# A graph network on one core: the last step of the last pair of batches by halves of the nodes, and the whole order of work drawn anew

## Chip, cores and metric

The kernel runs on one NeuronCore of one Trainium2 chip. The metric is the device time of one execution in microseconds (us), the median of several runs. Everything is in float32.

## What is computed

`x` has 32 batches of 512 nodes by 128 channels and `adj` is one 512 x 512 matrix, the same for all batches and used for both adjacencies of each layer. The reference, cut to what matters:

```python
# layer 0: x_1 stands for x; W[k] = weight of the k-th of 7 parts
parts = [x_1, adj x_1, adj^2 x_1, adj^3 x_1, adj x_1, adj^2 x_1, adj^3 x_1]
x = layernorm(x + sum_k parts[k] @ W[k])

# layer 1: five steps of a gated update, h starts as x
def step(h):
    m  = adj @ h                       # m_in and m_out are the same, since both matrices are adj
    av = concatenate([m, m])
    u3 = h @ u3_w.T + u3_b
    z  = sigmoid(av @ w3_w.T + w3_b + u3)
    r  = sigmoid(av @ w4_w.T + w4_b + u3)
    hv = tanh(av @ w5_w.T + w5_b + (r * h @ u5_w.T + u5_b))
    return (1 - z) * h + z * hv
x = layernorm(x + step^5(x))
```

## The kernel before

The 32 batches are 16 *pairs* (`q` = 0 to 15); each pair goes through layer 0 and then five steps (`s` = 0 to 4). The engines are TensorE (PE), VectorE (DVE), ScalarE (ACT), GpSimd (POOL) and SyncE (SP), the last of which only issues transfers. A float32 matmul is two PE instructions in the profile, so each count of PE instructions is twice that of the matmuls (transposes, L290, are one each).

**Products.** The products with `adj` (`pair_product`, `seven`, L380 to L550; L511 is the matmul line) take two batches together as a 2 x 2 block scheme with seven products in place of eight; the sums that it needs are made by POOL (L498) into `S`, and the results are put together by ACT (L372) and DVE (L376) from PSUM into the tiles `m`, one per batch. Layer 0 has similar products (L615, L749, L811).

**One step of one batch** (`gates`, L881): with channels on the partitions and the 512 nodes along the free dimension, `u3s` times `hT` is made in a PSUM bank of its own (L970) and copied with its bias to a tile `uT` by ACT (L975). Then PE makes `w4s m` (r), `w3s m` (z) and `w5s m` (h) in the banks `pr`, `pz`, `ph` (L888, 128 x 512 each). DVE adds bias and `uT` to the r and z banks (L893, L900), ACT takes the sigmoids (L895, L902), DVE makes `rh = r * h` (L896), PE adds `u5s rh` to the h bank (L888), ACT takes tanh (L909), DVE and POOL form the new `hT` (L921, L923, L925). The next product needs `h` with nodes on the partitions; `turn` (L332) does that through DRAM: a block transpose on DVE (L347), four stores issued by SP (L339), one fetch (L345). In the last two steps of the last two pairs (`ON_PE = {14: 2, 15: 2}`) it is done on PE instead (L1019, counted under L290, and a copy on ACT, L1022).

**The last step of pairs 14 and 15** is `quick`: ACT also makes 1 - z from the z bank (L914), DVE makes `(1 - z) h` and `z hv` (L916, L918), and `finish` (L928) lets PE sum three things in one bank by matmuls with the identity (L936): the batch's layer-0 result `h0`, `(1 - z) h` transposed, and `z hv` transposed, four blocks of 128 x 128 each.

**The norm** (`norm`, L292): for each block of 128 nodes two DVE instructions for mean and variance (L301, L302); then POOL, for all four blocks together, adds epsilon (L305), takes the power -1/2 (L308, 128 x 4), and makes the shift (L307, L310); then ACT applies it block by block (L318). For the very last tile DVE applies it (L314) and POOL leaves out the shift. SP stores the whole batch, 256 KB, with one transfer (L953).

**The order** is not written out by hand. `Plan` (L45) takes every operation with its engine, a duration, what it comes after, which buffers it takes and gives back, and a key. `run` goes through planned time: each engine that is free emits its ready operation of lowest key whose buffers are free. What it emits is each engine's order, fixed in the program. The keys are `KEYS[q]` for a pair plus 19 (`LONG`) per step, and small offsets inside a step. Besides real buffers there are tokens: `two` limits how many seven-product schemes are open at once, `inside` how many pairs.

Of the kernel before, what the change touches and what calls it, by code (L numbers as in the profile page):

```python
# [9 lines left out]
F32 = mybir.dt.float32  # L10
AF = mybir.ActivationFunctionType
ALU = mybir.AluOpType
PSUM = bass.MemoryType.PSUM

P = 128
NK = 4
N = NK * P
H = NK // 2
HN = N // 2
# [1 line left out]
NR = P // R  # L21
STEPS = 5
ON_PE = {14: 2, 15: 2}
KEYS = [8.0, 22.0, 60.0, 88.0, 108.0, 144.0, 174.0, 188.0, 210.0, 244.0, 274.0, 310.0, 338.0, 368.0, 384.0, 396.0]
LONG = 19.0
KEPT = 3
FIRST = 2
# [97 lines left out]
def gnn_resnorm_kernel(  # L125
# [17 lines left out]
    nc = tc.nc  # L143
    NP = x.shape[0] // 2
# [7 lines left out]
    def tiles(tag, n, shape=(P, N), pool=work):  # L152
        return [pool.tile(list(shape), F32, tag=f"{tag}_{i}", name=f"{tag}_{i}") for i in range(n)]
# [12 lines left out]
        hT=tiles("hT", 8),  # L166
        X=tiles("X", 3),
        uT=tiles("uT", 6),
        rh=tiles("rh", 2),
        z=tiles("z", 3),  # L170
        m=tiles("m", 5),
        S=tiles("S", 2, (P, 7, H, P)),
        v=tiles("v", 4),
        two=[None] * 3,
        inside=[None] * 14,
    )
    plan = Plan(slots)

    def chunk(k):
        return slice(k * P, (k + 1) * P)  # L180
# [49 lines left out]
    for i, n, of in (  # L230
# [8 lines left out]
        def emit(b11=b11, b12=b12, b21=b21, b22=b22, t=t):  # L239
            for j, (a, b) in enumerate(((b12, b11), (b22, t(0)), (b22, b12), (b21, t(1)))):  # L240
                nc.vector.tensor_tensor(t(j), a, b, ALU.subtract)  # L241
# [40 lines left out]
    ub3s, ub5s = plain(ub3, "ub3s"), plain(ub5, "ub5s")  # L282
    hv_b = const.tile([P, 1], F32, tag="hv_b", name="hv_b")
    hv_ready = plan("DVE", 0.1, lambda: nc.vector.tensor_tensor(hv_b, b5s, ub5s, ALU.add), after=ready, key=-30.0)
    weights = ready + [hv_ready]

    def transposes(dst, src_of):
# [1 line left out]
        for k in range(NK):  # L289
            nc.tensor.transpose(dst[:, chunk(k)], src_of(k), ident)  # L290

    def norm(n, name, src_of, dst_of, after, give, key, by_dve=False):  # L292

        mv = small.tile([P, n, 2], F32, tag="mv", name=f"mv_{name}")
        rstd = small.tile([P, n], F32, tag="rstd", name=f"rstd_{name}")
        shift = small.tile([P, n], F32, tag="shift", name=f"shift_{name}")
        got = []

        def moments(i):
            st = small.tile([P, 6], F32, tag="st", name=f"st_{name}_{i}")  # L300
            nc.vector.bn_stats(st, src_of(i))  # L301
            nc.vector.bn_aggr(mv[:, i, :], st)  # L302

        def power():
            nc.gpsimd.tensor_scalar(rstd, mv[:, :, 1], EPS, None, ALU.add)  # L305
            if not by_dve:
                nc.gpsimd.tensor_scalar(shift, mv[:, :, 0], -1.0, None, ALU.mult)  # L307
            nc.gpsimd.tensor_tensor(rstd, rstd, mhalf[:, :n], ALU.pow)  # L308
            if not by_dve:
                nc.gpsimd.tensor_tensor(shift, shift, rstd, ALU.mult)  # L310

        def apply(i):
            if by_dve:
                nc.vector.tensor_scalar(  # L314
                    dst_of(i), src_of(i), mv[:, i, 0:1], rstd[:, i : i + 1], ALU.subtract, ALU.mult
                )
                return
            nc.scalar.activation(  # L318
                dst_of(i), src_of(i), AF.Identity, bias=shift[:, i : i + 1], scale=rstd[:, i : i + 1]
            )  # L320

        for i in range(n):
            got.append(plan("DVE", 0.48, lambda i=i: moments(i), after=after, key=key))
        p = plan("POOL", 1.2 if by_dve else 1.75, power, after=got, key=key)
        engine, us = ("DVE", 0.35) if by_dve else ("ACT", 0.5)
        over = []
        for i in range(n):
            ends = give if i == n - 1 else []
            over.append(plan(engine, us, lambda i=i: apply(i), after=[p] + over, give=ends, key=key))
        return over  # L330

    def turn(src_of, dst_of, name, after, key, take=(), give=()):  # L332
# [548 lines left out]
    def gates(name, m, h, after, u_done, quick, key):  # L881
# [43 lines left out]
        emit = lambda: nc.gpsimd.tensor_tensor(plan[h], plan[z], plan[h], ALU.add)  # L925
        return plan("POOL", 1.27, emit, after=[t], give=[("z", z)], key=key + 0.8)

    def finish(q, b, name, h, parts, h0_of, after, key, done):  # L928

        bn, z = f"bt{name}", f"z{name}"  # L930
        y = lambda k: plan[bn][:, chunk(k)]

        def summed(tile, turned, first, last):
            for k in range(NK):
                a = tile(k)
                nc.tensor.matmul(  # L936
                    y(k),
                    lhsT=a if turned else ident,
                    rhs=ident if turned else a,
                    start=(first and k == 0),  # L940
                    stop=last,
                    skip_group_check=True,
                )

        keep, new = parts
        emit = lambda: summed(lambda k: h0_of(b)[:, k, :], False, True, False)
        t = plan("PE", 0.44, emit, after=list(after), take=[("bank", bn)], key=key)
        emit = lambda: summed(lambda k: plan[h][:, chunk(k)], True, False, False)
        t = plan("PE", 0.44, emit, after=[t, keep], give=[("hT", h)], key=key)
        emit = lambda: summed(lambda k: plan[z][:, chunk(k)], True, False, True)  # L950
        t = plan("PE", 0.44, emit, after=[t, new], give=[("z", z)], key=key)
        over = norm(NK, f"1_{2 * q + b}", y, lambda k: h0_of(b)[:, k, :], [t], [("bank", bn)], key + 10, q == NP - 1 and b == 1)
        emit = lambda: nc.sync.dma_start(out[2 * q + b].rearrange("(p k) c -> p k c", k=NK), h0_of(b))  # L953
        done.append(plan("SP", 0.36, emit, after=over, key=key + 10, late=2.0))

    def pair(q, key0):
# [6 lines left out]
        for s in range(STEPS):  # L963
            key = key0 + 30.0 + LONG * s
            name = f"{q}_{s}"
            last = s == STEPS - 1
            u_done = []
            for b in range(2):
                bn, uT = f"bv{name}_{b}", f"uT{name}_{b}"
                emit = lambda bn=bn, hb=h[b]: nc.tensor.matmul(  # L970
                    plan[bn], lhsT=u3s, rhs=plan[hb], start=True, stop=True
                )
                take = [("bank", bn), ("uT", uT)]
                p = plan("PE", 0.86, emit, after=h_done[b] + weights, take=take, key=key + 5)
                emit = lambda bn=bn, uT=uT: nc.scalar.activation(plan[uT], plan[bn], AF.Identity, bias=ub3s)  # L975
                u_done.append(plan("ACT", 0.69, emit, after=[p], give=[("bank", bn)], key=key + 5))
# [26 lines left out]
            for b in range(2):  # L1003
                nm = f"{name}_{b}"
                Xb = f"X{nm}"
                quick = last and not by_dma
                d = gates(nm, f"m{nm}", h[b], got[b], u_done[b], quick, key + 10)
                if quick:
                    finish(q, b, nm, h[b], d, h0_of, read[b], key + 15, done)
                    h_done.append(list(d))  # L1010
                    continue
                h_done.append([d])
                give = [("hT", h[b])] if last else []
                if by_dma:
                    h_of = lambda hb=h[b]: plan[hb].rearrange("p (k r l) -> p r k l", r=NR, k=NK)
                    t = turn(h_of, lambda Xb=Xb: plan[Xb], nm, [d] + read[b], key + 15, [("X", Xb)], give)
                else:
                    bn = f"bt{nm}"
                    emit = lambda bn=bn, hb=h[b]: transposes(plan[bn], lambda k: plan[hb][:, chunk(k)])  # L1019
                    take = [("bank", bn), ("X", Xb)]  # L1020
                    t = plan("PE", 0.44, emit, after=[d] + read[b], take=take, give=give, key=key + 15)
                    emit = lambda bn=bn, Xb=Xb: nc.scalar.copy(plan[Xb], plan[bn])  # L1022
                    t = plan("ACT", 0.59, emit, after=[t], give=[("bank", bn)], key=key + 15)
                after.append([t])
                if not last:
                    continue

                y = lambda b=b: h0_of(b)
                emit = lambda b=b, X_new=X_new, y=y: nc.gpsimd.tensor_tensor(
                    fit(y(), True), X_new(b), fit(y(), True), ALU.add  # L1030
                )
                ready = [t, fetched] if q < NP - KEPT else [t]
                t = plan("POOL", 1.27, emit, after=ready, give=[("X", Xb)], key=key + 17)
                i = 2 * q + b
                y_of = lambda k, y=y: y()[:, k, :]
                over = norm(NK, f"1_{i}", y_of, y_of, [t], [], key + 17)
                emit = lambda i=i, y=y: nc.sync.dma_start(out[i].rearrange("(p k) c -> p k c", k=NK), y())
                stored = plan("SP", 0.36, emit, after=over, key=key + 17, late=2.0)
                done.append(stored)
# [62 lines left out]
```

## Time and profile before

| | |
|---|---|
| median of 5 runs | 1511.73 us (1510.98 to 1512.60) |
| profiled execution | 1511.94 us |
| its span (first to last instruction) | 1510.1 us |
| TensorE clock granted, mean | 0.999 |
| PE / DVE / ACT / POOL busy | 99% / 68% / 50% / 56% of the span |
| matmuls of the gates and `u3s` (L888, L970) in the chain that ended last | 36.4% + 9.1% |
| products with `adj` (L511) in that chain | 32.9% |
| bytes moved by DMA | 142.91 MB, mean 95 GB/s |

In the profile's rows, "out<-in" names the tile written and the tiles read, without buffer numbers; "x16" is a count of instructions. The columns of a group are its total busy time and the mean of one instruction in nanoseconds, then the idle time of the engine just before them and what ended it. A row of waits gives the total, how often, and the longest. A row of the chain gives its start, its length and what ran. Ends of matmuls are modelled, so the time from one start to the next is the better measure of what one costs.

### The profile page before, as it was taken

The page shows a single profiled execution, that of the slowest core. Times are in us where ns is not written, and L with a number is a line of the kernel's source. Part 1 is how long each engine was busy: PE and PEld are TensorE (multiplying, and loading weights), DVE is VectorE, ACT ScalarE, POOL GpSimd, SP SyncE. Part 2 cuts the span into 40 slices and gives each one's busy share as a digit, 9 for nine tenths or more (in the row PEclk, how much of TensorE's full clock was granted, in tenths as well). Part 3 has the DMA queues.
Part 4 walks back from the last instruction along what each step waited for, and adds up shares of the span by engine and source line. Part 5 has one row for each costly group of instructions (what it writes and reads, how often), then busy time and mean ns, then how long its engine had stood idle before and what let it go on. Part 6 is the DMA issues. An engine that isn't in the chain of part 4 may idle for free.

```text
span 1510.1 us, 21208 instructions
## 1 busy us (share of the span) xinstructions
PE 1493.9 (99%) x6590; PEld 1045.4 (69%) x6590; DVE 1021.2 (68%) x2123; ACT 749.5 (50%) x1582; POOL 844.4 (56%) x1201
## 2 busy tenths in 40 slices
PE   8999999999999999999999999999999999999997
PEld 7877667667676767676767667677776776665665
DVE  5566676775776667665775766776578665767665
ACT  3354554455445545554454554554545544555454
POOL 4846754665545856663664655655665643544442
PEclk9999999999999999999999999999999999999999
DMA  3213334243333425233333443443343223433310
GB/s 96 71 57 98 100 88 113 79 123 99 98 112 91 119 81 144 80 110 91 98 98 98 119 114 89 111 133 92 98 106 102 80 70 80 108 102 82 84 36 35
DMA packets 165888, 142.91 MB, mean 95 GB/s; under 512 B 18960, under 2 KB 127504, under 8 KB 165776
## 3 DMA queue, kind: packets, MB, share of 16 engines
q1 hardware_dynamic: 165776, 141.57, 33.8%
q8 instruction: 52, 0.85, 0.2%
q14 instruction: 60, 0.49, 0.1%
HBM read 71.76 MB, written 69.73 MB: 94 GB/s over the span
## 4 chain that ended last, share of the span: by engine, by line
PE 98%; DVE 1%; DMA 0%; ACT 0%; POOL 0%; issue 0%; SPq 0%; POOLq 0%; DVEq 0%
PE bank L888 36%; PE bank L511 33%; PE bank L970 9%; PE bank L811 7%; PE bank L749 6%; PE bank L615 5%; PE bank L936 1%; PE bank L447 1%; PE bank L290 1%; DMA xg<-in_x 0%; DVE TT L241 0%; ACT h L318 0%; DVE h L440 0%; POOLq L1098 0%; DVE h L314 0%
## 5 line engine op out<-in xcount | busy, mean ns | idle before, releaser
L925 POOL TENSOR_TENSOR hT<-z,hT 128x512 f32<-128x512 f32 x156 | 198.3, 1276 | 256.9 <-DVE z L923 247.1
L511 PE MATMUL bank<-T,S 128*128 128x256 f32 x1232 | 307.0, 379 | 0.0
L511 PEld LDWEIGHTS bank<-T,S 128*128 128x128 f32 x1232 | 228.4, 190 | 74.9 <-ACT m L372 32.1
L372 ACT COPY m<-bank 128x256 f32<-128x256 f32 x320 | 119.3, 373 | 286.9 <-PE bank L511 285.0
L511 PE MATMUL bank<-at,S 128*128 128x256 f32 x824 | 211.2, 379 | 0.0
L511 PEld LDWEIGHTS bank<-at,S 128*128 128x128 f32 x824 | 153.5, 190 | 57.3 <-issue 37.1
L376 DVE TENSOR_TENSOR m<-bank,m 128x256 f32<-128x256 f32 x240 | 100.7, 420 | 120.3 <-PE bank L511 86.3
L921 DVE TENSOR_TENSOR bank<-bank,hT 128x512 f32<-128x512 f32 x156 | 108.3, 695 | 108.2 <-ACT bank L909 107.4
L888 PE MATMUL bank<-m,w4s 128*128 128x512 f32 x320 | 159.7, 592 | 0.0
L888 PE MATMUL bank<-m,w3s 128*128 128x512 f32 x320 | 157.4, 592 | 0.0
L888 PE MATMUL bank<-rh,u5s 128*128 128x512 f32 x320 | 156.9, 592 | 0.0
L970 PE MATMUL bank<-hT,u3s 128*128 128x512 f32 x320 | 156.5, 592 | 0.0
L893 DVE SCALAR_TENSOR_TENSOR bank<-bank,b4s,uT 128x512 f32<-128x512 f32 x160 | 119.9, 752 | 52.8 <-PE bank L888 48.5
L888 PE MATMUL bank<-m,w5s 128*128 128x512 f32 x320 | 155.0, 592 | 0.0
L909 ACT ACTIVATE bank<-bank,hv_b 128x512 f32<-128x512 f32 x160 | 105.5, 662 | 90.3 <-PE bank L888 89.0
L895 ACT ACTIVATE bank<-bank 128x512 f32<-128x512 f32 x160 | 93.2, 584 | 102.6 <-DVE bank L893 102.5
L975 ACT ACTIVATE uT<-bank,ub3s 128x512 f32<-128x512 f32 x160 | 109.8, 688 | 59.2 <-PE bank L970 58.0
L902 ACT ACTIVATE z<-bank 128x512 f32<-128x512 f32 x160 | 94.3, 596 | 64.8 <-DVE bank L900 60.6
L900 DVE SCALAR_TENSOR_TENSOR bank<-bank,b3s,uT 128x512 f32<-128x512 f32 x160 | 118.6, 752 | 11.3 <-PE bank L888 10.0
L347 DVE STREAM_TRANSPOSE v<-hT 128x512 f32<-128x512 f32 x152 | 105.7, 701 | 13.1 <-POOL hT L925 10.7
L896 DVE TENSOR_TENSOR rh<-bank,hT 128x512 f32<-128x512 f32 x160 | 107.5, 680 | 8.3 <-ACT bank L895 7.8
L376 DVE TENSOR_TENSOR UY<-bank,UY 128x256 f32<-128x256 f32 (+1 forms) x117 | 54.5, 467 | 81.1 <-PE bank L749 35.2
(163 smaller groups left out, 2503.7 us busy)
## 6 DMA issues: line engine op xcount, KB each, us to landing
d<-v SPq DMA_DIRECT2D x832, 64.0 KB, 1.8
X<-d SPq DMA_DIRECT2D x152, 256.0 KB, 2.7
v<-d SPq DMA_DIRECT2D x56, 256.0 KB, 2.8
xg<-in_x SPq DMA_DIRECT2D x32, 256.0 KB, 2.9
out<-h SPq DMA_DIRECT2D x32, 256.0 KB, 2.0
hd<-h SPq DMA_DIRECT2D x13, 512.0 KB, 3.8
h<-hd SPq DMA_DIRECT2D x13, 512.0 KB, 3.8
at<-in_adjT SPq DMA_DIRECT2D x4, 256.0 KB, 5.1
```

The costliest lines, as they stand in the source:

```text
L372: return "ACT", COPY[cols], lambda src: nc.scalar.copy(dst(i, j), src)
L376: return "DVE", ADD[cols], lambda src: nc.vector.tensor_tensor(dst(i, j), src, dst(i, j), ALU.add)
L511: nc.tensor.matmul(dst, lhsT=left[:, k, :], rhs=right[:, k, :], start=(first and k == 0), stop=(last and k == H - 1), skip_group_check=True,)
L811: nc.tensor.matmul(dst[:, chunk(j)], lhsT=left[:, k, chunk(j)], rhs=right[:, k, :], start=(first and j == k == 0), stop=(last and k == H - 1),
L888: mm = lambda dst, w, src, first, last: nc.tensor.matmul(plan[dst], lhsT=w, rhs=plan[src], start=first, stop=last)
L893: emit = lambda: nc.vector.scalar_tensor_tensor(plan[pr], plan[pr], b4s, plan[uT], ALU.add, ALU.add)
L896: emit = lambda: nc.vector.tensor_tensor(plan[rh], plan[pr], plan[h], ALU.mult)
L900: emit = lambda: nc.vector.scalar_tensor_tensor(plan[pz], plan[pz], b3s, plan[uT], ALU.add, ALU.add)
L921: emit = lambda: nc.vector.tensor_tensor(plan[ph], plan[ph], plan[h], ALU.subtract)
L925: emit = lambda: nc.gpsimd.tensor_tensor(plan[h], plan[z], plan[h], ALU.add)
L970: emit = lambda bn=bn, hb=h[b]: nc.tensor.matmul(plan[bn], lhsT=u3s, rhs=plan[hb], start=True, stop=True)
L975: emit = lambda bn=bn, uT=uT: nc.scalar.activation(plan[uT], plan[bn], AF.Identity, bias=ub3s)
```

## The change

Only the last step of pair 15 is computed in a new way, by two new functions; the norm gets a form for two tiles at once on ACT and DVE; the order of everything is drawn anew with other keys and other numbers of buffers and tokens.

- The `u3s` product is no longer made in a bank of its own and copied: it is the first matmul into the r bank and, a second time, into the z bank, and `w4s m` and `w3s m` are added to it there. The biases come in with the sigmoid on ACT, from three 128 x 1 tiles made once on DVE (`r_b`, `z_b`, and `k_b` = -`z_b` for 1 - z).
- Everything after these matmuls is done in two halves of 256 nodes: the sigmoids, `rh`, `u5s rh`, 1 - z, tanh, the products, the sum on PE (two banks in place of one), the norm (two blocks, so the power has 128 x 2), and the store (128 KB each, four in place of two).
- The first batch's `(1 - z) h` is made by POOL, the second's by DVE. The first batch's norm is applied by ACT and DVE, a block each; the second's by DVE.
- The two batches' gates have keys one apart, so that the second follows the first.
- `rh` has three buffers in place of two, `two` five tokens in place of three, `inside` thirteen in place of fourteen.

```diff
-KEYS = [8.0, 22.0, 60.0, 88.0, 108.0, 144.0, 174.0, 188.0, 210.0, 244.0, 274.0, 310.0, 338.0, 368.0, 384.0, 396.0]
+KEYS = [8.0, 22.0, 60.0, 88.0, 112.0, 144.0, 174.0, 180.0, 206.0, 244.0, 270.0, 286.0, 334.0, 366.0, 386.0, 398.0]
...
-        rh=tiles("rh", 2),
+        rh=tiles("rh", 3),
...
-        two=[None] * 3,
-        inside=[None] * 14,
+        two=[None] * 5,
+        inside=[None] * 13,
...
+    def last_biases():
+        nc.vector.tensor_tensor(r_b, b4s, ub3s, ALU.add)
+        nc.vector.tensor_tensor(z_b, b3s, ub3s, ALU.add)
+        nc.vector.tensor_scalar(k_b, z_b, -1.0, None, ALU.mult)
...
+    def last_gates(name, m, h, after, h_done, first, key):
+        rh, z, rest = f"rh{name}", f"z{name}", f"rest{name}"
+        pr, pz, ph = (f"b{g}{name}" for g in "rzh")
+        cols = [slice(g * HN, (g + 1) * HN) for g in range(2)]
...
+        ur = plan("PE", 0.86, lambda: mm(pr, u3s, h, True, False), after=h_done, take=[("bank", pr)], key=key)
+        uz = plan("PE", 0.86, lambda: mm(pz, u3s, h, True, False), after=h_done, take=[("bank", pz)], key=key + 0.5)
+        take = [("rh", rh), ("z", z)]
+        p = plan("PE", 0.86, lambda: mm(pr, w4s, m, False, True), after=after + [ur], take=take, key=key)
+        r = halves("ACT", 0.38, act(pr, pr, AF.Sigmoid, bias=r_b), [p], key)
+        r = halves("DVE", 0.42, times(rh, pr, h), [r], key, give=[("bank", pr)])
+        p2 = plan("PE", 0.86, lambda: mm(pz, w3s, m, False, True), after=[p, uz], key=key + 0.5)
+        zs = halves("ACT", 0.38, act(z, pz, AF.Sigmoid, bias=z_b), [p2], key + 0.5)
+        emit = lambda: mm(ph, w5s, m, True, False)
+        p3 = plan("PE", 0.86, emit, after=[p2], take=[("bank", ph)], give=[("m", m)], key=key + 0.7)
+        p4 = halves("PE", 0.43, lambda c: mm(ph, u5s, rh, False, True, c), [p3, r], key + 0.3, give=[("rh", rh)])
+        emit = act(rest, pz, AF.Sigmoid, scale=-1.0, bias=k_b)
+        k = halves("ACT", 0.38, emit, [p2], key + 0.55, [("rh", rest)], [("bank", pz)])
+        engine, us, by = ("POOL", 0.73, nc.gpsimd) if first else ("DVE", 0.42, nc.vector)
+        k = halves(engine, us, times(h, rest, h, by), [k, r, uz], key + 0.2, give=[("rh", rest)])
+        t = halves("ACT", 0.42, act(ph, ph, AF.Tanh, bias=hv_b), [p4], key + 0.4)
+        t = halves("DVE", 0.42, times(z, ph, z), [t, zs], key + 0.4, give=[("bank", ph)])
+        return k, t
...
+    def last_finish(q, b, name, h, parts, h0_of, after, key, done):
+        keep, new = parts
+        for g in range(2):
+            bn = f"bt{name}{g}"
...
+            t = plan("PE", 0.22, emit, after=list(after), take=[("bank", bn)], key=key + 0.6)
...
+            t = plan("PE", 0.22, emit, after=[t, keep[g]], key=key + 0.15)
...
+            t = plan("PE", 0.22, emit, after=[t, new[g]], key=key)
...
+            o = norm(H, f"1_{2 * q + b}_{g}", y, dst, [t], [("bank", bn)], key + 0.2, b == 1, b == 0)
...
+                nc.sync.dma_start(to[:, g * H : (g + 1) * H], h0_of(b)[:, g * H : (g + 1) * H])
...
-            u_done = []
-            for b in range(2):
+            u_done, h_before = [], h_done
+            ends_here = last and q == NP - 1 and ON_PE.get(q, 0) > 0
+            for b in range(0 if ends_here else 2):
...
+                if ends_here:
+                    d = last_gates(nm, f"m{nm}", h[b], got[b], h_before[b] + [biased], b == 0, key + 10 + b)
+                    last_finish(q, b, nm, h[b], d, h0_of, read[b], key + 10.2 + b, done)
+                    h_done.append(d[0] + d[1])
+                    continue
```

`halves` plans one operation twice, for columns 0 to 255 and 256 to 511, each half after the matching half of what it needs; `act` is an activation and `times` a product of those columns.

## The prediction

> **What bounds the kernel now.** I read the page (busy shares, slices, groups), then who PE waited for, then the chain that ended last in order of time, then the timeline of the last 70 us, and then how the two programs' instructions stand on each engine. From the page:
>
> ```profile
> PE 1493.9 (99%) x6590; PEld 1045.4 (69%) x6590; DVE 1021.2 (68%) x2123; ACT 749.5 (50%) x1582; POOL 844.4 (56%) x1201
> ...
> PE   8999999999999999999999999999999999999997
> ...
> L970 PE MATMUL bank<-hT,u3s 128*128 128x512 f32 x320 | 156.5, 592 | 0.0
> ...
> out<-h SPq DMA_DIRECT2D x32, 256.0 KB, 2.0
> ```
>
> From PE's waits, all of them:
>
> ```profile
> PE bank L290 <- DMA xg<-in_x: 4.7, 2, 3.6
> PE bank L749 <- DVE UY L376: 1.5, 1, 1.5
> PE bank L749 <- ACT UY L372: 0.9, 2, 0.5
> PE bank L290 <- ACT h L318: 0.4, 1, 0.4
> ```
>
> The reader is to see that PE has no idle time to give: 7.5 us of waits, all in the first 60 us (the timeline places them at 0 to 8, at 28 and at 52 to 57 us), then none until its last matmul. Every matmul removed or added after 60 us is therefore worth its full time, and work taken from DVE or ACT is worth nothing until PE has ended. What lies behind PE's end is in the chain:
>
> ```profile
> 1497.01 3.58 PE bank L936 x32
> ...
> 1500.62 0.31 DVE st L301
> ...
> 1502.42 0.23 POOL rstd L305
> ...
> 1502.96 1.01 POOL rstd L308
> ...
> 1504.33 0.23 POOL rstd L305
> ...
> 1504.61 1.09 POOLq L1098
> ...
> 1505.72 0.41 DVE h L314
> ```
>
> PE's last sum starts 16 instructions of 0.111 us at 1499.53, so PE ends at 1501.31. Behind it stand the statistics of both tiles, POOL's power of the first tile and then of the second, four DVE instructions to 1507.09, and a store: 3.01 us to the span's end at 1510.1. The tail behind PE is 8.8 us, the one place where this change can gain. The profiled execution took 1511.94, 1.84 over its span; the median of the runs, 1511.73, is 0.21 under it.
>
> **What the change does to PE's work.** Of the last step of pair 15 two `u3s` matmuls become four, since each tile's is now made in the r bank and again in the z bank. One costs two instructions 0.43 us apart (the chain has L888 x16 in 6.87 us; the row's 592 ns includes a modelled end): plus 2 x 0.86 = **+1.72 us**. Two `u5s` matmuls become four of half the width, and each sum of four 128-blocks two of two: the same columns (256 columns: 12 instructions in 2.59 us, so 0.216; twice that is 0.43), nothing. What falls away of uT (ACT, 0.69 each) and of the two additions per tile (DVE, 0.75 each) lay beside a busy PE: nothing. The three small bias instructions stand on DVE before the `at2` addition that starts at 31.22 after 1.92 us of idle time; 3 x 0.15 us (the hv_b row) fit into it: nothing. If that gap were gone, 0.45.
>
> **What the new order does.** PE's order is the same, row for row, over its first 198 rows, some 150 us, so the start keeps its 7.5 us. Behind that almost everything is reordered (KEYS, and the tokens of `rh`, `two` and `inside`), SP's and POOL's queues with it. For every matmul I set the PE time that stands in the drawn order between it and the matmuls whose results it needs against the sum of the rows between (for a transposed h: 0.2 to the reader, 0.66, 0.69, 0.69 on ACT and DVE, 1.27 on POOL, 0.70 on DVE, 1.76 of issues and 1.8 of landing, 0.34 and 2.7 of the fetch). Before, the tightest distance behind 60 us spares 0.03 us, and the trace has no wait. After, the tightest also spares 0.03, and only one is too short, in the last sum. So I put the middle at 0; this leaves out what waits in DVE's, POOL's and SP's queues behind another instruction, and that is the open price below.
>
> **The tail, walked in the order drawn.** With PE full, its last sum (z, second half of tile 1) would end at 1501.31 + 1.72 = 1503.03. The rows before it are, from the end: z first half (0.445), hT second half (0.445), `u5s` second half, which so ends at 1501.69. From there: 0.2 to ACT; tanh of a half 0.45 (0.66 for 512 columns; copies of 512 and 256 take 0.586 and 0.373, so half saves 0.21): 1502.34; DVE product 0.03 + 0.42: 1502.79; 0.05 to PE: 1502.84. PE is free at 1502.58, so it waits **0.26**, and ends at 1503.29. The first half's z ends at 1502.58, readable at 1502.78: its two statistics (four took 1.73) run 1502.82 to 1503.67, the second half's, behind them on DVE, to 1504.47. POOL: 0.08, 0.23, 0.08 and the power for the first half, then the same for the second. The power on 128x4 takes 1.04 while a product on 128x4 takes 0.20, so 0.84 is the function itself. On 128x2, which no row shows, it is between 0.23 (no more than a simple row) and 1.04; I take 0.62, half the 0.84 over 0.20, because at equal shape only the function differs. Then first half 1503.75 to 1504.68, second to 1505.69; 0.07 and two DVE instructions (four took 1.37): 1506.45. The store: 3.01, less 0.1 for 128 KB (64 KB land in 1.8, 256 KB in 2.0): span end **1509.35**. With the power at 1.04 both grow by 0.42 in a row: 1510.2. With 0.23 the second half's statistics come last instead: 1508.75. The same walk for tile 0 and for the r and z halves finds each product ready 0.3 us or more before PE's turn; DVE's second `rh` half stands behind tile 0's statistics and is ready at 1499.2, its matmul's turn being 1501.26.
>
> So the change buys some 2.5 us behind PE (two powers of half size, and no four-chunk statistics in front of them) and pays 1.72 + 0.26 for it on PE: −0.75.
>
> **Two rules.** The trace has the store of 256 KB landing in 2.0 us, and 64 KB in 1.8. The Trainium skill (SBUF — State Buffer, the DMA setup-cost knee) says a transfer costs about 2 us fixed plus its bytes at 436 GB/s; by that, four stores for two pay the fixed part twice as often, and the last one would be 0.3 us shorter, an estimate, in place of my 0.1. The trace has halves of 0.42 against 0.69 on DVE. The skill (Perfetto Trace Analysis, Optimizing Scalar/DVE Operations) lets instructions be broken up where those engines cause bubbles on others; PE has no bubbles here, so by this rule the halves in the gates are worth nothing before PE's end, as in my sum.
>
> **The rivals.**
> *A wait in the middle* (slower). A transposed h needs some 11 us from its `u5s` through ACT, DVE, POOL and SP. SP runs in order: a fetch waits for its four puts to land and holds the next tile's puts. The trace shows two fetches that occupied SP for 4.33 us (at 1459.33), hidden. If in the new order such a fetch stands ahead of puts whose tile PE needs next, and no other pair's matmuls are ready, PE stops for up to 4.3 us; +4.3 − 0.75 gives 1515.3. It decides once such waits sum to over 3.8 us. For it: tight distances, a new order everywhere, pairs 11 to 15 started at other keys. Against it: no wait in 1440 us before at the same tightness.
> *The halves give nothing* (no change): the power costs 1.04 on two columns, biased sigmoids are longer than I took, and each half's hand-over adds 0.1 to 0.3. The span is then 1510.2 to 1510.8, the time about 1512.
> *Faster by over 3 us*: the tail would have to lose 5 us of 8.8. It has statistics, power, two instructions and a store in line, 0.8 + 0.9 + 0.7 + 2.9 = 5.3 at the least after PE, so even with no wait 1503.03 + 5.3 = 1508.3 is the floor; only an unseen gain in the middle, where PE was full, could do it.
>
> **How the numbers follow.** About 0.2% (3 us) is what a measurement of this kernel can tell from no change. Forecast: span 1509.35, as profiled 1511.2, as a median 1511.0. Forecast and second rival together 0.83; a wait in the middle that decides 0.14; faster by over 3 us 0.03. Without the middle the bounds are 1508.75 to 1510.8 in span, 1510.4 to 1512.4 as a median, and with a little scatter of the runs (0.8 around the median) 1509.6 to 1513; the range reaches on towards the wait, to 1515.
>
> **What would show it.** Right: PE's waits beyond 60 us are under 1 us; `u3s` in the last step appears four times; PE ends 1.7 to 2.2 us later, the tail behind it is 6 to 7 us, the power on 128x2 reads near 0.62. Wrong: a wait of PE for S, X or hT between 150 and 1480 us (the first rival), a power of 1.04 (the second), or a PE busy time that has not grown by 1.7 us.

## The result, and the profile after

| | before | after |
|---|---|---|
| median | 1511.73 us (37 runs, 1510.59 to 1513.36) | 1515.0 us (19 runs, 1513.37 to 1517.0) |
| profiled execution | 1511.94 us, span 1510.1 | 1517.0 us, span 1515.2 |

The change makes the kernel slower by a factor of 1.0021, 95% interval [1.0015, 1.0027], some 3.3 us. The forecast was 1511.0. The profiled execution of after is the longest of its runs. The same kernel profiled once more (run `e6_changed_again`) has a span of 1512.0; most of the difference lies in the first 100 us, where x comes in, so the two traces of after are read side by side below. The lines of the page that answer to those shown of before:

```profile
PE 1498.7 (99%) x6598; PEld 1047.2 (69%) x6598; DVE 1021.9 (67%) x2128; ACT 750.6 (50%) x1586; POOL 848.8 (56%) x1209
...
L1075 PE MATMUL bank<-hT,u3s 128*128 128x512 f32 x316 | 155.4, 592 | 0.0
```

And of its DMA view:

```profile
out<-h SPq DMA_DIRECT2D x30, 256.0 KB, 2.1
...
out<-h SPq DMA_DIRECT2D x4, 128.0 KB, 1.7
```

PE has eight instructions more: four of 0.43 us each for the two added `u3s` matmuls, and four because the halves of `u5s` count twice. (The eight `u3s` instructions of the last step are not in the row of L1075; they stand on L948.) All the rows that PE waited for, as before (lines are numbered anew: L298 was L290, L761 was L749, L627 was L615, L523 was L511, L900 was L888; L1006 is the last step's sum):

```profile
PE bank L298 <- DMA xg<-in_x: 5.0, 2, 3.6
PE bank L761 <- DVE UY L388: 1.2, 1, 1.2
PE bank L1006 <- DVE z L973: 1.0, 1, 1.0
PE bank L761 <- ACT UY L384: 0.9, 2, 0.5
PE bank L627 <- DVE M L385: 0.9, 2, 0.6
PE bank L523 <- POOL S L510: 0.6, 1, 0.6
PE bank L298 <- ACT h L326: 0.4, 1, 0.4
PE bank L900 <- DVE rh L908: 0.2, 1, 0.2
```

The four rows of before are there with the same sum, 7.5 us. Four rows are new: one in the last step (1.0 for `z`), three in the middle (0.9 + 0.6 + 0.2). The end of the chain, which was two full powers of 1.01 and 1.04, is now:

```profile
1506.37 0.46 ACT bank L970
1506.85 0.46 ACT bank L970
...
1507.33 0.44 DVE z L973
...
1507.81 0.73 PE bank L1006 x4
1508.56 0.31 DVE st L309
...
1509.87 0.71 POOL rstd L316
...
1511.62 0.41 DVE h L322
```

Two things are to be seen. The tail behind PE did shrink: PE's last instruction starts at 1508.94 and the span ends 6.3 us later, 8.9 before. But in front of PE's last sums the chain leaves PE altogether, over two tanh halves one after the other and a product.

**Where the time went.** For every PE instruction I took the time from its start to the next one's, less 0.429 us for 512 columns, 0.216 for 256 and 0.111 for 128, which is what they take when nothing holds PE up. What is left over, in us (rounding in these three figures moves the second row by up to 0.7 us in every column alike, so differences between columns are what counts):

| | before | after | after again (`e6`) |
|---|---|---|---|
| 0 to 100 us | 8.6 | 9.9 | 7.2 |
| 100 to 1400 us | 1.1 | 3.7 | 3.1 |
| 1400 us to PE's end (the last step) | 0 | 2.04 | 2.04 |
| PE's last start to the span's end | 8.9 | 6.3 | 6.3 |

With the first 100 us left out, after minus before is +1.72 (the matmuls added) + 2.6 or 2.0 (middle) + 2.04 (last step) − 2.6 (tail behind PE) = 3.8 or 3.2, and the medians say 3.3. So two costs are missing from my sum: about 2 us in the last step and 2.0 to 2.6 us in the middle. In the first trace of after the middle has four places with more than 0.15 us left over: 0.76 before PE reads an `S` at 103 us, 0.41 before an `rh` at 939, and 0.74 and 0.49 before an `M` at 1016 and 1175. In the second trace the place at 103 is not there.

### The profile page after: what moved, and what is told of

Same layout as the page of the kernel before. It is cut to its first block, busy times and chain, and to the rows that moved or that the text cites. A ratio compares the mean times of both kernels' runs of the same rounds, so it can differ in the third digit from the quotient of the medians.

```text
span 1515.2 us, 21219 instructions
## 1 busy us (share of the span) xinstructions
PE 1498.7 (99%) x6598; PEld 1047.2 (69%) x6598; DVE 1021.9 (67%) x2128; ACT 750.6 (50%) x1586; POOL 848.8 (56%) x1209
## 4 chain that ended last, share of the span: by engine, by line
PE 96%; DVE 2%; DMA 1%; POOL 1%; ACT 0%; issue 0%; SPq 0%; POOLq 0%; DVEq 0%
PE bank L900 35%; PE bank L523 32%; PE bank L1075 9%; PE bank L823 7%; PE bank L761 6%; PE bank L627 5%; PE bank L948 1%; PE bank L459 1%; PE bank L298 1%; DMA xg<-in_x 0%; PE bank L1040 0%; PE bank L1006 0%; DMA d<-v 0%; DVE M L684 0%; POOL S L510 0%
## 5 line engine op out<-in xcount | busy, mean ns | idle before, releaser
L523 PE MATMUL bank<-T,S 128*128 128x256 f32 x1232 | 306.2, 380 | 0.6 <-POOL S L510 0.6
L523 PEld LDWEIGHTS bank<-T,S 128*128 128x128 f32 x1232 | 230.4, 190 | 78.1 <-ACT m L384 26.6
L523 PE MATMUL bank<-at,S 128*128 128x256 f32 x824 | 211.1, 379 | 0.0
L523 PEld LDWEIGHTS bank<-at,S 128*128 128x128 f32 x824 | 153.1, 190 | 55.9 <-issue 34.7
L900 PE MATMUL bank<-m,w4s 128*128 128x512 f32 x316 | 157.9, 592 | 0.0
L1075 PE MATMUL bank<-hT,u3s 128*128 128x512 f32 x316 | 155.4, 592 | 0.0
L900 PE MATMUL bank<-rh,u5s 128*128 128x512 f32 x316 | 155.0, 593 | 0.2 <-DVE rh L908 0.2
L900 PE MATMUL bank<-m,w3s 128*128 128x512 f32 x316 | 154.5, 592 | 0.0
L900 PE MATMUL bank<-m,w5s 128*128 128x512 f32 x316 | 153.1, 592 | 0.0
L935 DVE TENSOR_TENSOR z<-bank,z 128x512 f32<-128x512 f32 x156 | 105.4, 683 | 1.9
```

The costliest lines, as they stand in the source:

```text
L523: nc.tensor.matmul(dst, lhsT=left[:, k, :], rhs=right[:, k, :], start=(first and k == 0), stop=(last and k == H - 1), skip_group_check=True,)
L900: mm = lambda dst, w, src, first, last: nc.tensor.matmul(plan[dst], lhsT=w, rhs=plan[src], start=first, stop=last)
L1075: emit = lambda bn=bn, hb=h[b]: nc.tensor.matmul(plan[bn], lhsT=u3s, rhs=plan[hb], start=True, stop=True)
```

## The experiments

The theories: the last step's halves wait for each other, since a bank is waited for as a whole; the new order makes PE wait in the middle, whatever the last step does; and these waits in the middle come from sums on DVE and POOL that slow each other. The rivals: the added `u3s` work alone, or transfers in SP's queue.

### The order alone, and the step alone

```diff
# e1_order_alone, against after
-            ends_here = last and q == NP - 1 and ON_PE.get(q, 0) > 0
+            ends_here = False
# e2_step_alone, against after: the KEYS of before, and
-        rh=tiles("rh", 3),
+        rh=tiles("rh", 2),
-        two=[None] * 5,
-        inside=[None] * 13,
+        two=[None] * 3,
+        inside=[None] * 14,
```

> The changed kernel's keys and buffer counts with the last step of pair 15 as it was before (u3 in a bank of its own, whole tiles). Its PE order is the changed kernel's up to the last 25 rows. Theory O (the loss lies in the redrawn order, through short waits of PE in the middle where DVE's and POOL's sums run beside each other): about 1514.0 us, 2.3 over before, with waits of PE between 90 and 1200 us in the profile. Theory T (the loss lies in the last step, whose halves wait for each other because they share a PSUM bank): 1511.7, no waits of PE behind 60 us.

> The new last step by halves with the keys and buffer counts of before. Its PE order is that of before up to the last 25 rows. Theory O: about 1512.6 us, 0.9 over before (1.72 for the two added u3 matmuls, about 1.8 of waits in the last sums, less 2.6 that the tail behind PE gains), and no waits of PE from 60 us to the last step. Theory T: 1515, as the changed kernel.

Measured beside 1511.34 for before: the order alone 1512.84, ratio 1.0009 [1.0000, 1.0018]; the step alone 1511.37, ratio 1.0000 [0.9992, 1.0009]. By the table's measure the order alone loses 2.2 us in the middle (waits at 937, 1013 and 1172 us) and 0.08 in the last step; the step alone loses 0.75 and 0.72, and its tail behind PE is 6.5. Before has 1.1 and 0. So by the medians the new order costs some 1.5 us by itself, with an interval that just reaches no change; its trace has 1.1 us more in the middle than before. The new step by itself breaks even: +1.72 + 0.7 on PE against 2.4 behind it; so the added `u3s` work alone is not the loss. Neither run met an expected number: the order alone lies between the two that were set for it (1514.0 and 1511.7), and the step alone under both (1512.6 and 1515). The two together cost more than the sum of both, since the last step loses 2.04 in the new order and 0.72 in the old.

### A bank for each half

```diff
# e3_own_banks, against after; e5_step_alone_own_banks is the same edit on e2
-        pr, pz, ph = (f"b{g}{name}" for g in "rzh")
+        pr, pz = (f"b{g}{name}" for g in "rz")
+        ph = [f"bh{name}_{g}" for g in range(2)]
...
-        emit = lambda: mm(ph, w5s, m, True, False)
...
+        for g in range(2):
+            emit = lambda g=g: mm(ph[g], w5s, m, True, False, cols[g])
...   # u5s, tanh and the product of a half use that half's bank
```

> The changed kernel with the h bank of the last step split: each half of w5s m + u5s rh has a PSUM bank of its own, so that tanh of a half can start when its own matmul has ended. Both theories: the last wait of PE, 1.2 us in the changed kernel, falls to about 0.3 and the time by about 1.0, to 1514.0. If the wait has nothing to do with the shared bank: 1515, unchanged.

> The new last step with banks of its own for the halves of h, and the keys and buffer counts of before. Theory O: about 1511.5 us, level with before (the step alone at 1512.6, less 1.0). Theory T: 1514.

In the new order: 1512.13, ratio 1.0008 [0.9999, 1.0017]. After stood 3.3 us above before, this kernel stands 0.8 above it (the two intervals just touch, so it is the traces that decide); the last step's loss falls from 2.04 to 0.53 and the tail behind PE from 6.3 to 6.0, while the middle's loss, 2.9, is still 1.8 above that of before. The timeline of after, last step of the second tile (start, length, engine, line, what, and in brackets the idle time before it and what ended it):

```profile
1504.85 0.60 PE L948 MATMUL bank<-rh,u5s 128*128 128x256 f32 x2
...
1505.73 0.60 PE L948 MATMUL bank<-rh,u5s 128*128 128x256 f32 x2
...
1506.37 0.93 ACT L970 ACTIVATE bank<-bank,hv_b 128x256 f32<-128x256 f32 x2 [1.14 <-PE bank L948]
...
1507.33 0.42 DVE L973 TENSOR_TENSOR z<-bank,z 128x256 f32<-128x256 f32 x1 [1.64 <-ACT bank L970]
```

The same place with a bank for each half:

```profile
1500.67 1.03 PE L949 MATMUL bank<-rh,u5s 128*128 128x256 f32 x4
...
1501.30 0.88 ACT L971 ACTIVATE bank<-bank,hv_b 128x256 f32<-128x256 f32 x2
...
1501.78 0.43 DVE L974 TENSOR_TENSOR z<-bank,z 128x256 f32<-128x256 f32 x1 [0.93 <-ACT bank L971]
```

In after the first half's `u5s` is done at about 1505.3, but tanh of that half starts at 1506.37, 0.2 us behind the *second* half's matmul, and the first product starts only when both tanh halves are done (1506.37 + 0.93 = 1507.30). With own banks tanh starts 0.2 us behind the first half's matmul (1500.67 + 0.43 + 0.2), and the product behind the first tanh. That the halves wait for each other in a shared bank is so shown. What decides is the drawn order: in it, instructions of different engines on one bank run one after another. In after both `u5s` halves stand ahead of the first tanh. In the step alone, with the same shared bank and the old order, the first tanh stands ahead of the second `u5s`, and the wait is PE's:

```profile
1499.48 0.60 PE L948 MATMUL bank<-rh,u5s 128*128 128x256 f32 x2
...
1500.12 0.45 ACT L970 ACTIVATE bank<-bank,hv_b 128x256 f32<-128x256 f32 x1 [0.34 <-PE bank L948]
...
1500.62 0.30 PEld L948 LDWEIGHTS bank<-rh,u5s 128*128 128x128 f32 x2 [0.29 <-ACT bank L970]
```

There tanh starts 0.2 us behind the first half's matmul, and the second half's matmul 0.05 us behind the end of that tanh. So the last step with shared banks loses 0.72 in one order and 2.04 in the other. The halves of the SBUF tile `z` do not wait so: in after, DVE writes the second half of `z` from 1508.03 on, while PE's sum over the first half, which starts at 1507.81, still has a matmul to start at 1508.25. Whether the waits go by the bank or by the program's PSUM buffer is not shown here, since each buffer is one bank. The Trainium skill (PSUM — Partial Sum Buffer, PSUM bank collisions raise a hardware error) says that the compiler's scheduler ties together any two instructions on different engines which touch the same bank and the same 32 partitions, other columns or not; the waits here agree, and I had not used that rule.

On the old order the same edit is a miss: 1511.93, ratio 1.0003 [0.9994, 1.0012], no better than the step alone. PE's wait there is

```profile
PE bank L1014 <- DVE hT L974: 0.9, 1, 0.9
```

so the halves' waits were replaced by one for `(1 − z) h` of the second tile, which stood late in DVE's queue.

### The changed kernel again, and the slowed sums in the middle

`e6_changed_again` is after, unchanged. The others replace one line of the quad product (L684; L672 in before). Block transposes of the first operand then stand in place of the five 128x512 sums of each quad product, so that these instructions read one operand from SBUF where they read two. These kernels leave the sums out and do not compute the reference's result; only their time is of use:

```diff
# e7_order_one_input, against e1; e8_before_one_input, the same against before
-            emit = lambda: nc.vector.tensor_tensor(d(), a(), b(), ALU.add)
+            emit = lambda: nc.vector.transpose(d(), a())
```

> The changed kernel itself, beside the others, so that its loss is known on the same chip and its waits are seen in a second profile. Adding up the order alone (+1.5) and the waits of its own last step (1.72 of u3 and 1.85 of waits, less 2.65 behind PE, +0.9): about 2.4 over before. If the first measurement holds by itself: 3.3 over before.

> The redrawn order with the old last step, as in the run of the order alone, but the five sums of 128x512 that VectorE makes for every two pairs in layer 0 from two SBUF tiles are replaced by block transposes of one of the two tiles (this leaves those sums out); the instructions have the same place in every queue and about the same length (0.70 us). Theory C (VectorE's sums from two SBUF tiles and GpSimd's sums slow each other, which takes 0.5 us each from the path to PE): the waits of PE for M near 1013 and 1172 us go, the time falls by 1.0 to 1.4, to the level of before. Theory Q (the queues are too tight in the new order whatever the instructions take): the waits stay, 1.5 over before.

> Control: the kernel before with the same five sums replaced by block transposes (this leaves those sums out). Its sums are slowed as well, but no PE wait follows from it: theories C and Q both say no change, within 0.3 us of before.

Measured beside 1511.42: after again 1514.75, 1.0020 [1.0011, 1.0029]; the order with one input 1511.64, 1.0001 [0.9993, 1.0010]; before with one input 1511.12, 0.9998 [0.9989, 1.0007]. The order alone stood 1.5 above before and now stands 0.2 above it, while before itself hardly moves. Both waits for `M` are gone from the order's trace, which has 0.2 us more left over in the middle than before has; 0.25 us before an `rh` at 936.8 us are there still. The groups of after by shape (busy time, mean ns of one):

```profile
L684 DVE TENSOR_TENSOR M<-M,UY 128x512 f32<-128x512 f32 x21 | 19.3, 947 | 0.1
L684 DVE TENSOR_TENSOR M<-UY 128x512 f32<-128x512 f32 x7 | 7.6, 1084 | 0.0
```

and of the order with one input:

```profile
L684 DVE STREAM_TRANSPOSE M<-M 128x512 f32<-128x512 f32 x21 | 13.9, 689 | 0.1
```

Undisturbed, such a sum takes 0.69 too (in before the medians of its three groups are 0.68 to 0.73). Over 0.8 us took 15 of the 35 in before, 19 in after, 20 in the order alone, none with one input; each of the long ones ran beside an instruction of POOL. A transpose also has only one operand to wait for, but that is not what helps: DVE sat idle for 0.4 us in all before the 35 sums of after, and for as long before the 35 transposes. One place in the timeline of after shows what happens, and who pays:

```profile
1011.84 0.73 POOL L510 TENSOR_TENSOR S<-X 128x256 f32<-128x256 f32 x1 [7.69 <-DMA X<-d]
1011.93 1.18 DVE L684 TENSOR_TENSOR UY<-UY 128x512 f32<-128x512 f32 x1
...
1012.53 1.17 POOL L510 TENSOR_TENSOR S<-X,X 128x256 f32<-128x256 f32 x1
...
1013.03 1.21 DVE L684 TENSOR_TENSOR M<-UY 128x512 f32<-128x512 f32 x1
...
1015.66 0.55 DVE L385 TENSOR_TENSOR M<-bank,UY 128x384 f32<-128x384 f32 x1
...
1016.26 0.49 PE L627 MATMUL bank<-TT,SB 128*128 128x128 f32 x2 [0.57 <-DVE M L385]
```

DVE's addition into `M` (L385) stands behind the lengthened sums, and PE's next matmul needs that `M`. In before the sums are lengthened nearly as often, but there nobody waits for them.

### Both causes out at once

e10_both_out is after with both edits, a bank for each half and one input for the sums (so it, too, leaves the sums out).

> The changed kernel with both supposed causes taken out at once: each half of the last step's h has a bank of its own, and the five 128x512 sums of a quad product that read two tiles of SBUF on DVE read one (a transpose of the first operand in their place; that leaves those sums out, so only the time counts). If the two causes are the whole loss: the banks' own gain (about 2.5 from the changed kernel) and the sums' (1.2 between the two kernels with the new order) together bring the time back to within 0.5 us of the kernel before, 1511.0 to 1511.9, with no wait of PE for M or S over 0.3 in the middle. If something else in the new order costs time: 1512.5 or more, with waits of PE elsewhere.

Measured: 1511.31 beside 1511.76, ratio 0.9996 [0.9986, 1.0005]. The loss of 3.3 us is gone, within an interval of 1.4 us to either side. All of PE's waits in that kernel:

```profile
PE bank L298 <- DMA xg<-in_x: 3.7, 1, 3.7
PE bank L761 <- DVE UY L388: 1.4, 1, 1.4
PE bank L761 <- ACT UY L384: 0.9, 2, 0.5
PE bank L298 <- ACT h L326: 0.4, 1, 0.4
PE bank L1014 <- DVE hT L974: 0.2, 1, 0.2
```

No wait for `M`, `S` or `rh` is left between 100 and 1400 us (0.9 us left over by the table's measure), and 0.48 us in the last step. With the two costs removed the time is 1511.3, where my sum, which lacked them, had 1511.0. So they account for the whole loss, as far as this measurement can tell.

### Towards a better last step

These keep the old order.

```diff
# e9_u3_once, against e2: u3 h once for each tile, kept with its bias in uT, added to z on DVE
-        uz = plan("PE", 0.86, lambda: mm(pz, u3s, h, True, False), after=h_done, take=[("bank", pz)], key=key + 0.5)
+        uT = f"uT{name}"
+        emit = lambda: nc.scalar.activation(plan[uT], plan[pr], AF.Identity, bias=z_b)
+        uz = plan("ACT", 0.69, emit, after=[ur], take=[("uT", uT), ("bank", pz)], key=key + 0.5)
...
# e11_step_own_banks_pool, against e5; e12_u3_once_pool, against e9
-        engine, us, by = ("POOL", 0.73, nc.gpsimd) if first else ("DVE", 0.42, nc.vector)
+        engine, us, by = "POOL", 0.73, nc.gpsimd
# e13_product_early, against e12
-        t = halves("DVE", 0.42, times(z, ph, z), [t, zs], key + 0.4, give=[("bank", ph)])
+        t = halves("DVE", 0.42, times(z, ph, z), [t, zs], key - 1.0, give=[("bank", ph)])
```

> The new last step with the keys and buffer counts of before, but u3 h made once per tile: it stays in the r bank, and ACT copies it with its bias before w4s m is added there; VectorE adds the copy to the z bank in halves. PE loses two matmuls of 0.86 us. If PE's work is what the step pays with: 1.72 under the step alone, so about 1.4 under before, 1510.0. If the added VectorE sums of z make new waits in the last sums: level with before.

> The old order with the new last step, a bank for each half of h, and the product (1 - z) h on POOL for both tiles, not for the first alone. In the run with own banks and the old order PE waited 1.1 us for that product, which DVE made late behind its other work. If DVE's queue is the cause: the wait goes, and the time is about 0.9 lower than that run, some 0.3 below the kernel before (1510.7 to 1511.3). If POOL is late in its place (0.72 for each half, beside the powers of the other tile at 0.71): no gain, 1511.6 to 1512.3.

> The old order with the last step by halves, u3 h made once for each tile and added to z on DVE (so PE's added 1.72 is not there), and now the product (1 - z) h on POOL for both tiles. In the run with that product of the second tile on DVE, PE waited 1.3 us for it behind the first tile's statistics. If DVE's queue was the cause: the wait is gone and the time is 1.2 to 1.7 below the kernel before, 1509.7 to 1510.3, the whole gain that lay in the tail. If the chain is late in any case (sigmoid of 1 - z, then a product of 0.72 a half instead of 0.4): a wait of 0.5 to 1 stays, 1510.5 to 1511.2.

> The last run (old order, u3 h once for each tile, the product (1 - z) h on POOL) with one number changed: the second tile's product of z and tanh is due earlier, so DVE does its second half after two of the four statistics groups that it stood behind. In the last run PE waited 1.03 us for that half, in its place behind the statistics. If the wait was DVE's queue alone: it goes, PE ends about 1.0 earlier, and the time is some 2.0 to 2.4 below the kernel before, about 1509.3. If the statistics that it overtakes become late instead (they feed the powers on POOL, 0.71 each, and the last applications): the tail behind PE grows by 0.4 to 0.9 and the time stays at 1509.9 to 1510.4.

| | this | before beside it | ratio | PE's wait in the last step |
|---|---|---|---|---|
| e9 | 1511.09 | 1511.42 | 0.9996 [0.9988, 1.0005] | 1.3 for DVE's `(1 − z) h` |
| e11 | 1511.67 | 1511.76 | 1.0002 [0.9993, 1.0010] | 1.2 for POOL's `(1 − z) h` |
| e12 | 1510.38 | 1511.76 | 0.9991 [0.9982, 1.0000] | 0.9 for DVE's `z hv` |
| e13 | 1509.91 | 1511.03 | 0.9991 [0.9982, 1.0000] | none |

e9 was expected at 1510.0 if PE's work alone counted, and missed: the 1.72 us came off PE, and 1.3 went into a new wait. In e11 the product is late on POOL as well, since 1 − z of the second half left ACT only at 1501.98; the product starts at 1502.06. e12 gains 1.4 us, its interval just reaching 1.0. In e13 PE's wait is gone, and yet the gain is no larger: its tail behind PE is 7.45 us, 6.32 in e12. By the timeline of e13, POOL makes the four small norms one behind the other, with at most 0.1 us between two instructions, from 1498.81 to 1503.99 (5.18 us), its four powers of 0.71 to 0.72 among them; in e12 it does so from 1499.25 to 1504.42 (5.17 us). So the end is set by POOL's queue in both, and DVE's earlier product could not move it. e12 and e13 are the two best kernels of this study, about 0.1% under before; neither interval excludes no gain.

## Why the prediction was wrong, step by step

- **PE's added work, +1.72: right.** Eight instructions more, of the counts expected; taking the second `u3s` away (e9) let the last PE instruction start 0.5 us earlier than in e2 in spite of a wait of 1.3 there.
- **The start, 7.5 us of waits kept: right.** 5.0 + 1.2 + 0.9 + 0.4.
- **The tail behind PE: right.** 8.8 behind PE's end was to become 1509.35 − 1503.29 = 6.1; by last starts it went from 8.9 to 6.3. (The gain there is 2.7 in the walk, as its −0.75 has it; the "some 2.5" beside it is too low.) The power on 128x2 takes 0.71, taken as 0.62; from the last application's end (1511.62 + 0.73) to the span's end it is 2.85, taken as 2.9.
- **The walk of the last step, 0.26 of waiting: wrong, 2.04.** The step that failed is "0.2 to ACT; tanh of a half": I let each half wait for its own half, so that one tanh of 0.45 stood behind the last `u5s`. In the changed kernel two stand there, 0.93 together, and the first product behind both, because in the drawn order the halves' instructions on the shared bank follow each other. Own banks brought the loss to 0.53.
- **The middle at 0: wrong, 2.0 to 2.6.** The step that failed is the comparison of distances with durations from the rows. The tightest distance spared 0.03 us. The plan that draws the order has 0.69 for a DVE sum (L684) where rows of the same trace before had means of 857 to 934 ns, and such a mean is taken over sums of about 0.69 and sums of 0.8 to 1.6. Equal tightness was no argument either, since what counts is whether a tight place coincides with a lengthened sum. I had left the price of queues open, and most of it lay there: in DVE's queue, behind the lengthened sums.
- **The first rival** (a wait in the middle) came near in time, 1515.3, but not in cause. It named SP's fetch of 4.3 us in one piece; the runs show waits of 0.2 to 0.7 us behind DVE and POOL, and none behind a transfer after the start. **The second** (the halves give nothing) is wrong as put: the power did fall, and the biased halves of ACT took 0.45 to 0.49.
- **The rule on breaking up instructions** (Trainium skill, as cited in the prediction) was read as "worth nothing before PE's end". The trace says worse: halves in one bank moved the first result of the last step back and made bubbles on PE that were not there (2.04 us in after, none before).
- **Stores:** by issues and landings 128 KB take 1.7 us and 256 KB 2.0 (before) to 2.1 (after), a difference of 0.3 to 0.4, where I took 0.1 and the estimate from the skill's page was 0.3. On the path it is less: 3.01 became 2.85, so 0.16.

## What to carry to other kernels

Before walking a chain by halves, find out on which unit the waits are kept (here the PSUM bank): halves in one unit follow each other in the order drawn. A bank for each half took that wait away, but it paid in the new order alone; in the old one another wait took its place. When a new order is judged by distances between producer and consumer, use the longest duration in a group, not its mean, and mark the instructions whose durations fall into two groups. A part of a change that breaks even alone (the new step) and one that costs a little alone (the new order) can cost more together, so take a composite change apart.

## What the runs showed of the hardware

A DVE sum of two SBUF tiles (128x512) and a POOL sum (128x256) take turns. In the rows of after from 1011.84 on, POOL's sum runs undisturbed to 1012.57; DVE's ends 0.54 later, at 1013.11; POOL's next ends 0.59 after that, at 1013.70; DVE's next 0.54 after that, at 1014.24. Alone they take 0.69 and 0.73, so about 0.15 of each runs beside the other, and the rest is waiting for the turn. A DVE transpose with one input keeps its 0.69. The Trainium skill (SBUF — State Buffer, Who interferes with whom) states that a DVE instruction with two SBUF inputs contends with a GpSimd instruction that reads SBUF, that the contention is an exclusive lock, and that a DVE instruction with at most one SBUF input, outside the modes that use both ports, does not contend. The runs agree, except for the 0.15 that overlaps.

POOL's power falls from 1.04 on 128x4 to 0.71 on 128x2, where a product takes 0.20 on either shape: 0.33 for two columns fewer, and by the same slope some 0.38 that does not depend on them (an estimate from these two rows).
